# Another list of how many positions of each step are summed by twos, in a graph layer on one core

## The chip, the core and the metric

The kernel runs on one core of a Trainium2 chip. The metric is the device time of one execution in microseconds (us), as the median of several runs. The profile is of one further execution.

## What is computed

The reference normalizes the node features, sums the attributes of the edges that arrive at each node, and puts both through two dense layers:

```
h = maximum(layernorm(x), 0)                       # x: 12500 x 128
agg = segment_sum(edge_attr, dst)                  # 412500 x 48 -> 12500 x 48, dst sorted
z = relu(concat([h, agg, globals_of_graph_0]) @ W1 + b1)      # 256 hidden
out = x + z @ W2 + b2                              # 12500 x 128
```

All is in float32. The edges are 79 MB and make up most of what is read.

## The kernel before

**Steps.** The sorted edges are cut into chunks of CE = 896 (128 partitions x T = 7 positions). CS = 8 chunks make a step; there are NS = 58 steps, 57 full ones and a last short one. A step has two halves of CH = 4 chunks. For each chunk and position a one-hot matrix says which of W = 32 nodes near the chunk's start each edge belongs to. VectorE makes these matrices (`onehot`, line 312), two steps ahead (EARLY = 2).

**Sums.** `aggregate(s, h, twos)` multiplies, on TensorE, one-hot matrix by edge attributes, and adds the results up in PSUM (`ps`). A position of a half can be taken in two ways. One by one: four products, each with a 32-column stationary operand and 48 moving columns, each into its own 32 partitions. By twos: two products, each with the one-hot matrices of two neighbouring chunks as a 64-column stationary operand and the attributes of both as 96 moving columns; two of the four blocks that come out are wanted, the others are not read. The program issues 56 products for a step with no position by twos and 28 for one with all 14 by twos; the trace records two matmuls and two weight loads for a product, so 112 and 56.

**Levels.** `LEVELS[s]`, line 608, says how many of the step's 14 positions (7 in each half) are taken by twos:

```
twos = [max(0, LEVELS[s] - T), min(T, LEVELS[s])]     # first half, second half
```

So up to 7 the second half alone is concerned, and within a half the last positions are. Where a half has any, `keep_sums` (line 360) makes two further small copies on ScalarE besides the usual one, since the second chunk of a pair has its sums in the other 48 columns.

**What follows a step's sums.** ScalarE copies them to SBUF (`sums`). `place_columns` makes on VectorE a matrix that says where each of the 128 rows belongs among the nodes, `place` multiplies on TensorE (`pp`), and `add` adds on VectorE into the node sums `aggT` (line 391). Blocks of up to 512 nodes whose sums are complete go through the two layers in pieces (`turn`, `first_h`, `first_a`, `relu`, `second`, `result`, `store`), which a planner with costs spreads over half-steps (`piece`, `at`). The planner does not look at LEVELS: the order of all engines is written out under a manual schedule and is the same for any list.

**Loads.** Each step has four loads of edges of 336 KB (`load(s, i)`, line 144 issues them on SyncE's queue). `few` makes each of them wait until the load FLIGHT = 5 places before it has landed, and until the product that TensorE was given last at that point of the program is done. They are issued three steps ahead (AHEAD = 4). Loads of node rows (`xt`) and of indices (`di`) go through the same rule.

Of the kernel before, what the change touches and what calls it, by code (L numbers as in the profile page):

```python
# [22 lines left out]
def kernel(  # L23
# [134 lines left out]
    with fast:  # L158
# [175 lines left out]
        def aggregate(s, h, twos):  # L334
            left = s == NSF and h
            if h == 0:
                banks_s[s] = ps_agg.tile([P, 512], F32, name="ps")[:, :4 * DE].rearrange("p (h f) -> p h f", h=2)
            ps, es, oh = banks_s[s], edges[s], onehots[s]
            n = TT if left else T
            for t in range(n):  # L340
                first, end = t == 0 and h == 0, t == n - 1
                if t >= n - twos:
                    for q in range(0, CH, 2):
                        c = CH * h + q
                        product(ps[W * q:W * (q + 2), h], oh[:, c // 2, t], both[s][c // 2][:, :, t * DE:(t + 1) * DE],
                                start=first, stop=end, skip_group_check=True)
                    continue
                for q in range(1 if left else CH):
                    c = CH * h + q
                    o = DE * (q % 2) if twos else 0  # L350
                    product(
                        ps[W * q:W * (q + 1), h, o:o + DE], oh[:, c // 2, t, c % 2], es[c][:, t * DE:(t + 1) * DE],
                        start=first, stop=end, skip_group_check=True)
# [32 lines left out]
        def add(s):  # L386
            _, v = nc.values_load_multi_w_load_instructions(  # L387
                at_i[0:1, s:s + 1], engines=[DVE], min_val=low(s), max_val=high(s),
                skip_runtime_bounds_check_because="clamped to these on the chip")
            to = aggT[:HI + DE, ds(v[0], WG)]  # L390
            nc.vector.tensor_tensor(to, to, banks_p.pop(s)[:HI + DE, :WG], OP.add)  # L391
# [213 lines left out]
        FLIGHT = 5  # L605


        LEVELS = (0, 0, 0, 0, 7, 0, 0, 9, 14, 3, 14, 14, 0, 14, 3, 3, 2, 0, 5, 14, 0, 14, 2, 3, 0, 4, 14, 0, 14, 2, 4, 0, 3, 0, 5, 14, 0, 14, 0, 4, 0, 2, 0, 3, 14, 0, 14, 4, 2, 2, 0, 2, 2, 4, 0, 0, 0, 0)
        LATE = NS - 7
        NEAR = len(FIRST) + 1  # L610
        with tc.manual_schedule():
# [242 lines left out]
            for s in range(NS):  # L854
# [27 lines left out]
                if s >= LATE:  # L882
                    for p in now:
                        place(p)
                        add(p)
                twos = [max(0, LEVELS[s] - T), min(T, LEVELS[s])]
                aggregate(s, 0, twos[0])
# [175 lines left out]
```

## Time and profile before

| | |
|---|---|
| median of 3 runs | 300.12 us |
| the runs | 300.12, 307.49, 296.84 us |
| the profiled execution | 298.43 us |
| its span, first to last instruction | 296.6 us |
| mean granted TensorE clock | 0.991 |
| moved by DMA | 95.19 MB, 321 GB/s mean |

How to read it: PE is TensorE's products, PEld its weight loads, DVE VectorE, ACT ScalarE, POOL GpSimd, SP SyncE. A row names line, engine, operation, output and inputs. Every product of the kernel is issued through one helper, so its line is L195, and the tile name tells them apart: `ps` are the sums by one-hot matrices, `pp` the placement, `ph` the first layer, `po` the second, `pt` transposes. "issue" as the end of a wait means that the profile shows nothing that the engine waited for. The clock is the share of TensorE's full clock that was granted.

### The profile page before, as it was taken

To read this page: it belongs to the slowest core of one execution; us is meant where nothing else is said; L and a number is where in the kernel's file an instruction comes from. 1 tells how busy PE (TensorE), PEld (TensorE's weight loads), DVE (VectorE), ACT (ScalarE), POOL (GpSimd) and SP (SyncE) were. 2 spreads that over 40 slices of the span, in tenths; PEclk is the share of its full clock that TensorE was granted. 3 is DMA by queue.
4 is the path that set the end of the run, shared out by engine and by line. 5 is a ranking of instruction groups with operands and counts; after the bars stand their busy time and mean duration, and the time that the engine had idled before them with its cause. 6 is when DMAs were issued, how large, how long until landed. Compare 5 with 4: busy or idle time off the path is not lost.

```text
span 296.6 us, 15062 instructions
## 1 busy us (share of the span) xinstructions
PE 283.1 (95%) x6553; PEld 223.5 (75%) x6554; DVE 237.0 (80%) x537; ACT 161.0 (54%) x399; POOL 73.7 (25%) x88
## 2 busy tenths in 40 slices
PE   6799897999999999999999999999999999999992
PEld 2657666898878778878878788867877977787781
DVE  6838969699998997887978699698986799986222
ACT  3477557323756664743666458644651985664420
POOL 3032381130212563021022212021111022103720
PEclk9999998999999999999999999999999999999998
DMA  6999999999999999999999999999999999999962
GB/s 162 372 314 345 272 358 313 370 370 370 356 357 356 326 367 285 298 348 290 332 312 339 346 345 317 336 321 322 310 347 337 353 298 323 337 352 317 363 222 81
DMA packets 69815, 95.19 MB, mean 321 GB/s; under 512 B 5018, under 2 KB 64739, under 8 KB 69743
## 3 DMA queue, kind: packets, MB, share of 16 engines
q1 hardware_dynamic: 67583, 87.66, 89.1%
q0 software_dynamic: 2160, 6.50, 6.1%
q8 instruction: 53, 0.87, 1.2%
q14 instruction: 19, 0.16, 0.1%
HBM read 87.74 MB, written 6.40 MB: 317 GB/s over the span
## 4 chain that ended last, share of the span: by engine, by line
PE 81%; DVE 8%; ACT 3%; DMA 2%; issue 2%; SPq 1%; DVEq 1%
PE ps L195 30%; PE ph L195 21%; PE po L195 14%; PE pp L195 10%; PE pt L199 5%; DVE oh L312 3%; DMA e<-in_edge_attr_dram 2%; DVE place L374 2%; ACT xn L438 1%; ACT hT L452 1%; PE pt L195 1%; DVE st L408 1%; DVE aggT L391 1%; DVE ph L489 1%; DVEq L387 1%
## 5 line engine op out<-in xcount | busy, mean ns | idle before, releaser
L312 DVE TENSOR_TENSOR oh<-iota,rel 128x1792 f32<-128x1792 f32 (+1 forms) x60 | 120.5, 2009 | 0.4 <-ACT rel L270 0.4
L195 PEld LDWEIGHTS ps<-e,oh 128*32 128x32 f32 (+1 forms) x5448 | 94.7, 116 | 21.7 <-issue 5.8
L195 PE MATMUL ps<-e,oh 128*32 128x48 f32 (+1 forms) x5448 | 106.5, 217 | 3.1 <-issue 1.2
L360 ACT COPY sums<-ps 128x192 f32<-128x192 f32 (+2 forms) x129 | 36.7, 285 | 78.7 <-PE ps L195 76.8
L431 POOL TENSOR_TENSOR xb<-xt,b_sb 128x512 f32<-128x512 f32 (+1 forms) x21 | 34.2, 1630 | 131.7 <-DVE aggT L533 79.4
L195 PE MATMUL ph<-hT,w1h 128*128 128x512 f32 (+2 forms) x100 | 49.6, 602 | 0.1
L195 PE MATMUL po<-w,hid 128*128 128x128 f32 (+1 forms) x376 | 48.0, 281 | 0.9 <-ACT hid L516 0.9
L516 ACT ACTIVATE hid<-ph,bias 128x512 f32<-128x512 f32 (+2 forms) x49 | 30.4, 670 | 30.4 <-PE ph L195 22.9
L195 PEld LDWEIGHTS po<-w,hid 128*128 128x128 f32 (+1 forms) x376 | 45.1, 196 | 2.0 <-ACT hid L516 1.3
L391 DVE TENSOR_TENSOR aggT<-aggT,pp 112x246 f32 x58 | 23.6, 406 | 24.5 <-PE pp L195 18.2
L195 PE MATMUL pp<-place,sums 128*112 128x128 f32 x232 | 39.0, 291 | 0.2 <-DVE place L374 0.2
L195 PEld LDWEIGHTS pp<-place,sums 128*112 128x112 f32 x232 | 28.9, 176 | 7.1 <-issue 1.7
L438 ACT ACTIVATE xn<-xt,sh,sc 128x128 f32<-128x128 f32 x80 | 33.1, 483 | 0.3
L374 DVE TENSOR_TENSOR place<-iota,pos 128x256 f32<-128x256 f32 x58 | 32.9, 569 | 0.0
L195 PE MATMUL ph<-aggT,w1a 48*128 48x256 f32 (+1 forms) x192 | 28.6, 402 | 0.2 <-DVE aggT L391 0.2
L195 PEld LDWEIGHTS ph<-aggT,w1a 48*128 48x128 f32 x192 | 17.2, 186 | 10.1 <-issue 6.8
L452 ACT COPY hT<-pt 128x512 f32<-128x512 f32 (+1 forms) x22 | 23.0, 1044 | 3.2 <-PE pt L199 3.1
L195 PEld LDWEIGHTS ph<-hT,w1h 128*128 128x128 f32 x100 | 16.7, 196 | 7.1 <-issue 4.6
L533 DVE TENSOR_TENSOR aggT<-po,xb 128x512 f32<-128x512 f32 x16 | 11.0, 685 | 9.2 <-PE po L195 9.2
L541 POOL DMA_DIRECT2D out_dram<-ot x9 | 5.0, 553 | 51.6 <-DVE ot L533 43.7
L408 DVE BATCH_NORM_STATS2 st<-xt 128x6 f32<-128x128 f32 x80 | 17.3, 277 | 0.0
L199 PE MATMUL pt<-ident,xn 128*128 128x128 f32 x84 | 14.1, 289 | 0.0
(137 smaller groups left out, 188.1 us busy)
## 6 DMA issues: line engine op xcount, KB each, us to landing
e<-in_edge_attr_dram SPq DMA_DIRECT2D x230, 336.0 KB, 5.2
xt<-in_x_dram SPq DMA_DIRECT2D x19, 256.0 KB, 4.9
out_dram<-aggT POOLq DMA_DIRECT2D x16, 256.0 KB, 4.5
out_dram<-ot POOLq DMA_DIRECT2D x7, 256.0 KB, 4.8
di<-in_dst_dram SPq DMA_DIRECT2D x3, 448.0 KB, 5.3
aggT<-in_x_dram SPq DMA_DIRECT2D x4, 256.0 KB, 4.2
xt<-in_x_dram SPq DMA_DIRECT2D x2, 128.0 KB, 4.6
out_dram<-ot SPq DMA_DIRECT2D x2, 128.0 KB, 3.3
```

Source lines behind the costliest of these rows:

```text
L195: last[:] = [nc.tensor.matmul(*a, **k).ins.name]
L199: last[:] = [nc.tensor.transpose(*a, **k).ins.name]
L312: nc.vector.tensor_tensor(to, iota[:, None, :W].to_broadcast([P, n, W]), r[:, :, None].to_broadcast([P, n, W]), OP.is_equal)
L360: nc.scalar.copy(to[k, h], ps[k, h, None, o:o + DE].to_broadcast([k.stop - k.start, h.stop - h.start, 2, DE]))
L374: nc.vector.tensor_tensor(po, iota[:, None, :WP].to_broadcast([P, 2, WP]), pos[:, s, :, None].to_broadcast([P, 2, WP]), OP.is_equal)
L391: nc.vector.tensor_tensor(to, to, banks_p.pop(s)[:HI + DE, :WG], OP.add)
L408: nc.vector.bn_stats(st[:m, q, :], xs[j][:m, q, :])
L431: nc.gpsimd.tensor_tensor(xb[:m, :r], xs[j][:m, :r], b2_sb[:m, None, :].to_broadcast([m, r, D]), OP.add)
L438: nc.scalar.activation(xn[:m, q], xs[j][:m, q], AF.Relu, bias=shift[j][:m, q:q + 1], scale=scale[j][:m, q:q + 1])
L452: nc.scalar.copy(hT[:, :m * r].rearrange("d (p r) -> d r p", r=r), ht[j][:, :m * r].rearrange("d (r p) -> d r p", r=r))
L516: nc.scalar.activation(to, ph, AF.Relu, bias=bias[:, h:h + 1])
L533: nc.vector.tensor_tensor(ot[:m, :r], pos_o[j][:m, :r], xbs[j][:m, :r], OP.add)
```

## The change

One tuple is replaced. Nothing else is touched.

```diff
-        LEVELS = (0, 0, 0, 0, 7, 0, 0, 9, 14, 3, 14, 14, 0, 14, 3, 3, 2, 0, 5, 14, 0, 14, 2, 3, 0, 4, 14, 0, 14, 2, 4, 0, 3, 0, 5, 14, 0, 14, 0, 4, 0, 2, 0, 3, 14, 0, 14, 4, 2, 2, 0, 2, 2, 4, 0, 0, 0, 0)
+        LEVELS = (0, 0, 0, 0, 11, 4, 14, 3, 14, 14, 0, 14, 3, 2, 0, 2, 0, 0, 3, 0, 2, 0, 2, 0, 1, 3, 0, 0, 0, 3, 0, 0, 1, 0, 3, 0, 4, 0, 14, 0, 14, 4, 2, 3, 0, 0, 2, 0, 14, 0, 14, 5, 2, 4, 1, 2, 1, 0)
```

The sum of the list goes from 248 to 185. Steps with any position by twos go from 35 to 33, steps with all 14 from 12 to 8, and mixed steps (1 to 13) from 23 to 25. By stretches of steps:

| steps | positions by twos before | after |
|---|---|---|
| 4 to 9 | 33 | 60 |
| 10 to 36 | 148 | 43 |
| 37 to 57 | 67 | 82 |

## The prediction

> **What bounds the kernel now.** I read the page first (busy shares, the 40 slices, the chain that ended last), then stretches of time with the granted clock, then what SyncE's queue waited for, and last the chain of waits in a few windows, to price one step's sums.
>
> ```profile
> PE 283.1 (95%) x6553; PEld 223.5 (75%) x6554; DVE 237.0 (80%) x537; ACT 161.0 (54%) x399; POOL 73.7 (25%) x88
> DMA  6999999999999999999999999999999999999962
> q8 instruction: 53, 0.87, 1.2%
> PE 81%; DVE 8%; ACT 3%; DMA 2%; issue 2%; SPq 1%; DVEq 1%
> e<-in_edge_attr_dram SPq DMA_DIRECT2D x230, 336.0 KB, 5.2
> ```
>
> Two resources are full at once: TensorE is busy for 95% of the span, and the DMA engines show 9 in 37 of 40 slices. The chain follows TensorE, so TensorE looks like the bound. Stretches of time (length; busy time of PE, PEld, DVE, ACT and POOL; clock; DMA share; GB/s) say the same of the middle:
>
> ```profile
> 45.70:49.10 3.40, 1.81 (x52) 1.44 (x40) 3.40 (x7) 1.83 (x4) 0.33 (x1) 1.00 0.96 314
> 49.10:52.60 3.50, 3.50 (x54) 3.27 (x53) 3.50 (x4) 2.47 (x8) 0.74 (x2) 0.51 0.93 291
> 140.00:185.00 45.00, 45.00 (x1067) 35.88 (x1071) 38.13 (x84) 28.65 (x71) 8.66 (x7) 1.00 1.01 333
> 185.00:230.00 45.00, 45.00 (x1132) 35.54 (x1120) 37.15 (x76) 20.99 (x50) 6.64 (x6) 1.00 0.99 329
> ```
>
> From 140 to 230 us TensorE has no idle time. But the loads are no freer. A load of edges waits until the fifth load before it has landed, and until TensorE has reached a named product. The queue's waits show which of the two binds:
>
> ```profile
> SPq L144 <- DMA e<-in_edge_attr_dram: 108.2, 176, 2.4
> SPq L144 <- PE pp L195: 6.5, 15, 1.1
> ```
>
> 176 of the 230 loads were let go by the landing of an edge load; the largest group let go by a product is 15. So the loads run as one closed stream that TensorE hardly paces, and sums by twos fill TensorE's time beside it. The question is how far TensorE runs behind its data, since only that much can be won by lightening TensorE.
>
> **The price of a position.** Steps around 110 to 120 us in the chain (start, length, matmul records):
>
> ```profile
> 110.06 1.33 PE ps L195 x112
> 114.23 2.46 PE ps L195 x56
> 119.03 1.64 PE ps L195 x104
> ```
>
> Level 0 takes 1.33 us with 112 records, level 14 takes 2.46 us with 56. So a position by twos costs (2.46 - 1.33) / 14 = 0.081 us more, although it saves 4 matmul records and as many weight loads. Level 2 (x104) took 0.31 us more, not 0.16: a mixed step pays 0.15 us once. The new list has 63 positions fewer (5.1 us less) and 25 mixed steps for 23 (0.3 us more): 4.8 us less work on TensorE. The order of all else stays.
>
> ScalarE copies twice more in each step that has any twos, 33 steps for 35, four copies fewer; at 54% busy it hides them. VectorE, GpSimd and SyncE issue the same instructions in the same order. VectorE (45-us stretches with 37 to 38 us busy) has room for the few microseconds by which TensorE may come earlier.
>
> **Steps 4 to 9.** Levels 11, 4, 14, 3, 14, 14 replace 7, 0, 0, 9, 14, 3: 27 positions more, 27 x 0.081 = 2.2 us. They land where TensorE stood idle:
>
> ```profile
> 41.46 0.29 PE L195 MATMUL ps<-e,oh 128*32 128x48 f32 x8 [0.35 <-issue]
> 46.86 0.37 PE L195 MATMUL ps<-e,oh 128*32 128x48 f32 x13 [0.81 <-issue]
> 48.62 3.28 PE L195 MATMUL po<-w,hid 128*128 128x128 f32 x16 [0.77 <-ACT hid L516]
> 59.02 1.95 PE L195 MATMUL po<-w,hid 128*128 128x128 f32 x16
> ```
>
> That is 1.93 us idle. Right behind it the clock was 0.51 for 3.5 us (second stretch above), and 16 products that take 1.95 us at 59.02 took 3.28. With steps 5 and 6 fuller the idle time closes and the clock should hold: 3.5 x 0.49 = 1.7 us come back. TensorE would gain 1.93 + 1.7 - 2.2 = 1.4 us here. I carry none of it, because the next part caps what TensorE gains before step 37.
>
> The Trainium skill's page "TensorE: Matmul & The Clock Gate" (HAM oscillation) asks for no idle gap over about 3.4 us; by it no gap here would lower the clock. The trace decides otherwise: the longest gap above is 0.81 us, and the clock fell after a stretch with 1.81 of 3.40 us busy. By the page the new waits below cost only themselves; by the row, a stretch half idle can cost 1.7 us more, which the range takes in.
>
> **Up to step 37: the data bind.** Steps 4 to 36 hold 78 positions fewer: 78 x 0.081 = 6.3 us. How much can TensorE use? Step 37's sums, and the last of its four loads (the 152nd of 230):
>
> ```profile
> 188.12 2.53 PE L195 MATMUL ps<-e,oh 128*64 128x96 f32 x56
> L144 SPq DMA_DIRECT2D e<-in_edge_attr_dram x1: 502/502/502, 182.3 to 182.3; - x1
> DMA to landing us min/median/max: 4.8/4.8/4.8
> ```
>
> It landed at 182.3 + 4.8 = 187.1. Step 37 now has level 0, and its second half, which needs this load, comes 1.33 / 2 = 0.7 us after its start: it can start at 186.4, 1.7 us sooner than 188.1. The other 4.6 of the 6.3 us become waits for edges in steps 10 to 36, in the place of the work. What queues behind such a wait on TensorE is the same step's placement and the layer's products; VectorE's additions then come as late as those.
>
> **The stream itself.** Fewer twos mean more instructions, and TensorE's instructions come over the same DMA engines: 53 packets of 0.87 MB in all (16 KB each) for 6553 + 6554 records, one for about 250. Their time is 1.2% x 16 x 296.6 / 53 = 1.07 us each on one engine. One began at 113.4, and the load issued just before it:
>
> ```profile
> L144 SPq DMA_DIRECT2D e<-in_edge_attr_dram x1: 367/367/367, 113.3 to 113.3; - x1
> DMA to landing us min/median/max: 6.4/6.4/6.4
> q8 instruction: 1, 0.02, 2.3%
> ```
>
> It took 6.4 us against a median of 5.2: the packet held up the stream by about its own length. Each position not taken by twos adds 8 records. Up to step 37 that is 78 x 8 / 250 = 2.5 packets, 2.5 x 1.0 = 2.5 us of stream; for the whole list 63 x 8 / 250 = 2.0. The bounds of one packet are 0 (wholly beside the loads) and 1.2 us (6.4 - 5.2); I take 1.0, nearest to its own 1.07. So step 37 starts -1.7 + 2.5 = +0.8 us against before.
>
> The Trainium skill's page "Runtime: NRT & Kernel Launch" (Instruction fetch mechanics) calls crossing a 16 KB block of instructions mostly hidden; then step 37 starts 1.7 us early. The load at 113.3 speaks against it; it is the first rival below.
>
> **From step 37 to the end.** The list has 15 positions more here (-63 against -78) and one mixed step more: 15 x 0.081 + 0.15 = 1.4 us. The tightest place is step 51:
>
> ```profile
> 253.73 1.71 PE L195 MATMUL ps<-e,oh 128*32 128x48 f32 x104
> L144 SPq DMA_DIRECT2D e<-in_edge_attr_dram x1: 368/368/368, 247.8 to 247.8; - x1
> DMA to landing us min/median/max: 5.2/5.2/5.2
> ```
>
> Its last load (the 208th) landed at 253.0 and binds 0.7 us into the step: 252.3, 1.4 us of room. Later by 70 x 8 / 250 = 2.2 packets it would start at +0.8; TensorE's own way from step 37 gives +0.8 + 8 x 0.081 = +1.4 there. TensorE binds. Sum: 0.8 + 1.4 = +2.2 us.
>
> The profiled execution took 298.4 us (span 296.6 and 1.8 around it): 300.6. The median of the runs shown is 300.1, 1.7 us above; on it the forecast is 302.3 us.
>
> **The rivals.**
>
> First, the instruction packets cost the loads nothing. Then -1.7 + 1.4 = -0.3 us: 298.1 on the profile, 299.8 on the median. For it: one engine in sixteen is held. Against: the load at 113.3. Chance 0.2.
>
> Second, TensorE is the bound after all and takes all the relief: 4.8 us of work less, 1.93 us of idle time filled and 1.7 us of clock regained, -8.4 us: 290.0 on the profile, 291.7 on the median, faster by 2.8%. For it: 45.00 of 45.00 us busy. Against: the landings of step 37 and step 51, 1.0 and 0.7 us ahead of the sums. It decides only if the stream too comes over 6 us sooner, and nothing in the change hastens it. Chance 0.06.
>
> Third, slower: TensorE runs out of instructions. At 41.46 and 46.86, in steps 5 and 6, both at level 0, it stopped for 0.35 and 0.81 us within its sums, with "issue" as what ended it and not a landing, and the clock drop followed: 1.2 + 1.7 = 2.9 us for the group. The new list puts low steps in rows at 15 to 17, 20 to 24, 26 to 28 and 30 to 33. The waits for edges up to step 37 (4.6 us, and 2.5 more with the later stream) would swallow 7.1 us of such stops. Four groups are 11.6 us: 2.2 + 11.6 - 7.1 = 6.7 us, 306.8 on the median. Three give 303.9, so it decides from the fourth group on, or sooner where one falls behind step 37 (44 and 45 are both at 0) and nothing swallows it. Against: from 140 to 230 us TensorE stood still nowhere (45.00 of 45.00), with a dozen steps at level 0 or 2 among them. Chance 0.16.
>
> **How the numbers follow.** Within 2% (294.1 to 306.1; about what a measurement of this kernel can tell, its three runs lying between 296.8 and 307.5) lie my forecast, 0.58, and the first rival, 0.2: 0.78. Faster 0.06, slower 0.16. The likeliest time is 302.3. The range reaches down to 296.5 (the first rival, less the 3.3 us by which the fastest run shown lies below the median) and up to 307.0 (the forecast, two clock drops of 1.7 us that nothing absorbs and 2.5 x 0.2 us for packets at their upper bound make 306.2; the third rival's 306.8 is taken in, its worse ends are not).
>
> **What would show it.** Right: a shorter busy time of TensorE by some 5 us, idle stretches that end with a landing of edges between 100 and 150 us, 55 instruction packets, a clock near 1.00 at 49 to 53 us, and sums of step 37 starting within 1 us of the landing of its last load. Wrong: TensorE still without idle time and the span shorter by over 3 us (second rival); gaps inside the sums of steps at level 0 to 3 that no landing ends, with a clock of 0.5 behind them (third); an end before 299 us with 55 packets (first).

## The result, and the profile after

| | before | after |
|---|---|---|
| median of 6 runs each | 299.38 us (296.84 to 307.49) | 307.78 us (305.36 to 308.90) |
| ratio, with 95% interval | | 1.031 (1.024 to 1.038) |
| profiled execution, its span | 298.43 us, 296.6 us | 307.25 us, 305.4 us |

The changed kernel is slower by 3.1%, 5.5 us above the forecast and 0.8 us above the range. Ratios here leave out disturbed runs, so they can differ a little from the quotient of two medians.

From the page of the changed kernel: busy times, instruction packets, the chain that ended last, and the groups of TensorE's sums and of the second layer.

```profile
PE 281.6 (92%) x6805; PEld 218.7 (72%) x6806; DVE 236.4 (77%) x537; ACT 158.5 (52%) x395; POOL 74.6 (24%) x88
q8 instruction: 55, 0.90, 1.2%
PE 81%; issue 6%; DVE 4%; ACT 3%; DMA 2%; SPq 1%; DVEq 1%
L195 PE MATMUL ps<-e,oh 128*32 128x48 f32 (+1 forms) x5700 | 103.0, 214 | 6.4 <-issue 4.9
L195 PE MATMUL po<-w,hid 128*128 128x128 f32 (+1 forms) x376 | 48.7, 279 | 5.9 <-issue 4.6
```

The same two groups in the kernel before:

```profile
L195 PE MATMUL ps<-e,oh 128*32 128x48 f32 (+1 forms) x5448 | 106.5, 217 | 3.1 <-issue 1.2
L195 PE MATMUL po<-w,hid 128*128 128x128 f32 (+1 forms) x376 | 48.0, 281 | 0.9 <-ACT hid L516 0.9
```

TensorE is busy for 1.5 us less than before (283.1), and the span is 8.8 us longer, so its idle time grew by 10.3 us, from 13.5 to 23.8. The chain shows where to look: "issue", time in which the engine waited for nothing that the profile shows, rose from 2% to 6%. What TensorE waited for, in the changed kernel (total, times, longest; rows that differ little between the kernels are left out):

```profile
PE ps L195 <- issue: 4.9, 8, 1.3
PE po L195 <- issue: 4.6, 6, 1.3
PE ps L195 <- DMA e<-in_edge_attr_dram: 1.4, 3, 0.5
PE pt L195 <- issue: 1.2, 1, 1.2
PE ph L195 <- DVE ot L533: 0.6, 1, 0.6
PE ph L195 <- issue: 0.2, 1, 0.2
```

and in the kernel before:

```profile
PE ps L195 <- issue: 1.2, 2, 0.8
PE ps L195 <- DMA e<-in_edge_attr_dram: 0.9, 2, 0.5
```

Stops by "issue" went from 2 (1.2 us) to 16 (4.9 + 4.6 + 1.2 + 0.2 = 10.9 us), that is +9.7. With the 0.6 us put down to VectorE, which falls in the same pattern, as shown next, that is the 10.3 us; all other waits together changed by less than 1 us. Waits for edges, which the forecast expected to grow by 4.6 us, grew by 0.5.

**What the stops have in common.** I numbered all records of TensorE in order of start: matmuls, weight loads, and the 133 of its sequencer, semaphores for the most part, which the busy counts leave out. All 16 stops, and the one put down to VectorE (at 99.43), stand at a count that leaves 192 when divided by 256, to within three records. So do the two of before, at 41.46 and 46.86. (Why 192, the traces don't show.) Three in a row in the changed kernel (start, length, operation, idle time before):

```profile
140.22 1.35 PE L195 MATMUL ps<-e,oh 128*32 128x48 f32 x106 [0.38 <-issue]
...
145.00 1.32 PE L195 MATMUL ps<-e,oh 128*32 128x48 f32 x105 [0.67 <-issue]
...
149.69 0.38 PE L195 MATMUL po<-w,hid 128*128 128x128 f32 x1 [0.64 <-issue]
```

The first two stand inside the sums of a step each, the third inside a second layer. What they share is the distance (length; busy time and records of PE and PEld, the other engines; clock; DMA):

```profile
140.22:145.00 4.78, 4.11 (x127) 2.78 (x127) 4.75 (x12) 2.71 (x7) 0.68 (x1) 1.00 1.01 338
145.00:149.69 4.69, 4.05 (x129) 3.79 (x128) 4.17 (x16) 2.01 (x4) 0.00 (x0) 1.00 1.02 339
```

With two semaphore instructions more in the first stretch, and one record less at an edge of the second, 127 + 127 and 129 + 128 are 256 instructions each, one 16 KB packet. The packets of the instruction queue that belong to them are found by narrow windows, here 137.7 to 137.8, 142.5 to 142.6 and 147.3 to 147.4 us; each row is the packet that began there, and its time as a share of 16 engines for 0.1 us:

```profile
q8 instruction: 1, 0.02, 62.8%
...
q8 instruction: 1, 0.02, 59.5%
...
q8 instruction: 1, 0.02, 58.2%
```

They took 0.628 x 16 x 0.1 = 1.00, 0.95 and 0.93 us, so they ended at 138.8, 143.5 and 148.3, and TensorE went on 1.4 to 1.5 us later each time. The next packet began 2.3 us after TensorE had gone on (140.22 to 142.55, 145.00 to 147.35). 2.3 + 0.95 + 1.45 = 4.7 us is the whole period here. A block that TensorE can do in 4.1 us takes 4.7, and TensorE stops at its end. Over all 17 stops the time from packet's end to going on is 1.25 to 1.6 us. The period is less fixed: the packet begins 1.9 to 3.6 us after TensorE passed the block end before (median 2.7), and the block before a stop takes 4.6 to 6.0 us (median 5.2).

The strongest sign takes in all block ends, with or without a stop. I paired packets and block ends one by one, in order. No block end is passed sooner than 1.25 us after its packet ended, in either kernel. In the kernel before 4 of 50 are passed within 1.65 us of it, the median being 2.9; in the changed kernel 26 of 52. So the packet is not merely a load on the DMA engines, as the prediction's sum had it: TensorE waits for it. And packets do not run ahead: in the changed kernel each begins from 1.3 us ahead of the passing of the block end before to 3.6 us behind it.

How near the limit each kernel is can be read from one window, 140 to 190 us, first before, then after:

```profile
140.00:190.00 50.00, 50.00 (x1197) 40.13 (x1199) 42.57 (x92) 31.39 (x75) 8.66 (x7) 1.00 1.01 333
```

```profile
140.00:190.00 50.00, 45.93 (x1365) 36.10 (x1364) 41.12 (x91) 26.30 (x63) 9.22 (x7) 1.00 0.96 312
```

Before, 1197 + 1199 records pass in 50 us, 5.3 us for 256. After, 1365 + 1364 pass, 4.7 us for 256, which is the period above, and 4.07 us are idle. It is no sharp limit: eleven single blocks of the kernel before went by in 3.3 to 4.7 us without a stop.

**Where it is lost.** The sums of step 9 start 2.1 us earlier than before (58.83 for 60.90), those of step 16 1.8 us earlier (88.27 for 90.09), those of step 37 4.3 us later and those of step 57 8.7 us later (290.34 for 281.66). The early steps gained, steps 16 to 37 lost 6.1 us and the rest 4.4 us. The data were there. Step 37's last load and its sums, in the changed kernel:

```profile
L144 SPq DMA_DIRECT2D e<-in_edge_attr_dram x1: 367/367/367, 182.0 to 182.0; - x1
...
DMA to landing us min/median/max: 5.3/5.3/5.3
```

```profile
192.43 0.38 PE L195 MATMUL ps<-e,oh 128*32 128x48 f32 x16
194.06 0.63 PE L195 MATMUL ps<-e,oh 128*32 128x48 f32 x41 [1.26 <-issue]
```

It landed at 187.3, 0.2 us later than before, and was first needed over 5 us after that.

### The profile page after: what moved, and what is told of

Read it like the earlier page. It is cut to its first block, busy times and chain, and to the rows that moved or that the text cites. A ratio compares the mean times of both kernels' runs of the same rounds, so it can differ in the third digit from the quotient of the medians.

```text
span 305.4 us, 15564 instructions
## 1 busy us (share of the span) xinstructions
PE 281.6 (92%) x6805; PEld 218.7 (72%) x6806; DVE 236.4 (77%) x537; ACT 158.5 (52%) x395; POOL 74.6 (24%) x88
## 4 chain that ended last, share of the span: by engine, by line
PE 81%; issue 6%; DVE 4%; ACT 3%; DMA 2%; SPq 1%; DVEq 1%
PE ps L195 30%; PE ph L195 21%; PE po L195 15%; PE pp L195 10%; PE pt L199 4%; DMA e<-in_edge_attr_dram 2%; DVE place L374 1%; PE pt L195 1%; ACT xn L438 1%; ACT hT L452 1%; ACT hid L516 1%; DVE oh L312 1%; DVE ot L533 1%; SPq L144 0%; DVEq L387 0%
## 5 line engine op out<-in xcount | busy, mean ns | idle before, releaser
L195 PEld LDWEIGHTS ps<-e,oh 128*32 128x32 f32 (+1 forms) x5700 | 90.3, 114 | 26.0 <-issue 8.8
L195 PE MATMUL ps<-e,oh 128*32 128x48 f32 (+1 forms) x5700 | 103.0, 214 | 6.4 <-issue 4.9
L360 ACT COPY sums<-ps 128x192 f32<-128x192 f32 (+2 forms) x125 | 35.3, 284 | 91.3 <-PE ps L195 89.8
L431 POOL TENSOR_TENSOR xb<-xt,b_sb 128x512 f32<-128x512 f32 (+1 forms) x21 | 35.2, 1675 | 138.7 <-DVE aggT L533 99.3
L195 PE MATMUL po<-w,hid 128*128 128x128 f32 (+1 forms) x376 | 48.7, 279 | 5.9 <-issue 4.6
L374 DVE TENSOR_TENSOR place<-iota,pos 128x256 f32<-128x256 f32 x58 | 31.1, 538 | 0.0
L195 PE MATMUL ph<-aggT,w1a 48*128 48x256 f32 (+1 forms) x192 | 29.3, 404 | 0.8 <-DVE ot L533 0.6
L195 PEld LDWEIGHTS ph<-aggT,w1a 48*128 48x128 f32 x192 | 17.2, 186 | 11.5 <-issue 8.4
L533 DVE TENSOR_TENSOR aggT<-po,xb 128x512 f32<-128x512 f32 x16 | 11.0, 687 | 11.5 <-PE po L195 11.5
```

Source lines behind the costliest of these rows:

```text
L195: last[:] = [nc.tensor.matmul(*a, **k).ins.name]
L360: nc.scalar.copy(to[k, h], ps[k, h, None, o:o + DE].to_broadcast([k.stop - k.start, h.stop - h.start, 2, DE]))
L374: nc.vector.tensor_tensor(po, iota[:, None, :WP].to_broadcast([P, 2, WP]), pos[:, s, :, None].to_broadcast([P, 2, WP]), OP.is_equal)
L431: nc.gpsimd.tensor_tensor(xb[:m, :r], xs[j][:m, :r], b2_sb[:m, None, :].to_broadcast([m, r, D]), OP.add)
L533: nc.vector.tensor_tensor(ot[:m, :r], pos_o[j][:m, :r], xbs[j][:m, :r], OP.add)
```

## The experiments

Theory S (supply): TensorE's instructions come in blocks of 256, at most about one ahead; where TensorE uses a block up in less than about 4.7 us it stops at the block's end, so the time depends on how many records there are and on which of them share a block. Theory D (data and array): the edge stream and the array's own work bind, as in the sum on record, and the stops are a by-product. A third possibility, that the old list is simply better in itself wherever the block ends fall, came up on the way.

| run | list and change | median, us | ratio (95%) | stops by "issue", us |
|---|---|---|---|---|
| early | new list in steps 0 to 15, old after | 301.75 | 1.007 (1.000 to 1.014) | 5, 3.4 |
| late | old list in steps 0 to 15, new after | 307.66 | 1.016 (1.005 to 1.027) | 17, 13.3 |
| zero | no position by twos | 322.60 | 1.074 (1.065 to 1.083) | 34, 33.8 |
| apart | old list, 116 of its pairs as two half-wide products each | 315.95 | 1.051 (1.040 to 1.061) | 9, 9.1 |
| spread | 185 positions, otherwise placed | 304.04 | 1.007 (0.999 to 1.015) | 13, 11.6 |
| paced | 251 positions, placed by block | 302.29 | 0.996 (0.990 to 1.001) | 3, 2.8 |
| flight4 | new list, 4 loads in flight | 331.68 | 1.088 (1.073 to 1.102) | none |
| flight8 | old list, 8 loads in flight | 305.51 | 1.016 (1.009 to 1.023) | 9, 8.0 |
| grid | new list, 64 records put ahead | 321.99 (one run) | - | 22, 21.3 |
| gridold | old list, 64 records put ahead | 312.70 | 1.038 (1.022 to 1.054) | 15, 11.8 |
| grid256 | new list, 256 records put ahead | 311.41 | 1.027 (1.010 to 1.044) | 19, 15.3 |

Stops (number, total) are those of the profiled execution of each, which can lie some microseconds off its median.

**Which part of the list.** The two halves of the change, alone:

```diff
 late:  LEVELS = old[0:16] + new[16:58]
 early: LEVELS = new[0:16] + old[16:58]
```

> The old list up to step 15, the new one from step 16 on. Theory (instruction supply): a block of 256 of TensorE's instructions comes no sooner than some 4.8 us after the block before it was entered, so low levels in a row make TensorE stop at block ends; the stops of the new list lie at steps 16 to 37, so this kernel keeps them: 306 to 311 us, with ten or more stops ended by issue. Rival (later stream of edges, as forecast): 300 to 303, waits ended by landings. Rival (the longer sums in steps 4 to 9 are the loss): 298 to 300.

> The new list up to step 15, the old one from step 16 on. Instruction supply: stops only up to step 16 or so (two or three, 1 to 2 us), and the idle time and the low clock near 46 to 52 us are gone: 296 to 300 us, no different from before or up to 1% faster. Rival (steps 4 to 9 are the loss): 306 to 309. Rival (later stream of edges): 299 to 301.

Late loses about half of the 3.1% by its ratio (1.005 to 1.027). Early, expected between no change and 1% faster, is at 1.000 to 1.014. The intervals overlap, so the times alone do not split the loss. The stops do: 16 of late's 17 lie from step 16 on. Both lists have 81 positions in steps 0 to 15, so late has the changed kernel's records and block ends from step 16 on, and ten of its stops stand at the very block ends where the changed kernel stops. So most stops come from steps 16 on, where positions were taken away, and not from the 27 added in steps 4 to 9. For the same reason early has the instructions and block ends of before from step 16 on; yet it has 5 stops there (3.4 us), where before has none. So the place of the block ends is not all: it also matters when TensorE reaches an end and when its packet comes. Which of the two made these five is not shown, nor how much the number of stops varies between executions of one kernel.

**More supply needed, less array work.** All levels at zero:

```diff
-        LEVELS = (0, 0, 0, 0, 7, 0, 0, 9, 14, 3, ...)
+        LEVELS = (0,) * 58
```

> No position by twos anywhere: TensorE has 248 x 0.08 = 20 us less to do than before and some 2000 instructions more, 59 blocks for 51. Instruction supply: 53 blocks at 4.8 us from 41 us on end at 295, and the ends of steps need 10 us more: 305 at the least, 310 to 318 with blocks that no stop makes up for. Rival (TensorE's time decides): under 295. Rival (later stream of edges): 8 packets of 1 us less 2 us of room, 304 to 306, with waits ended by landings.

```profile
PE 272.4 (85%) x7545; PEld 212.6 (66%) x7546; DVE 236.9 (74%) x537; ACT 140.6 (44%) x329; POOL 72.7 (23%) x88
PE 77%; issue 12%; ACT 5%; DMA 2%; DVE 1%; SPq 1%; DVEq 0%; ACTq 0%
```

```profile
PE ps L195 <- issue: 32.4, 33, 3.3
PE ps L195 <- DMA e<-in_edge_attr_dram: 1.9, 3, 1.1
```

TensorE is busy for 10.7 us less (20 were expected; for 20 us in four stretches its clock is at half, which lengthens the work), the waits for edges are 1.9 us, and the kernel is 7.4% slower, with 33.8 us of stops. At 322.6 us it is above the 310 to 318 expected. Theory D has nothing to put this down to. A window far from the start shows the limit again: 1315 + 1313 records in 50 us, 4.9 us for 256.

```profile
100.00:150.00 50.00, 45.76 (x1315) 34.95 (x1313) 39.35 (x83) 22.49 (x53) 17.79 (x13) 1.00 0.98 323
```

The attempt at the converse, more records at the same array work, failed:

```diff
+    for v in (0, 1) if apart_ else (None,):   # one half of the 96 columns each
-        product(ps[W * q:W * (q + 2), h], oh[:, c // 2, t], both[...][:, :, ...], ...)
+        product(ps[W * q:W * (q + 2), h, cols], oh[:, c // 2, t], both[...][:, two, ...], ...)
```

> The old list, and TensorE's array time with it, but in steps 10 to 36 the 116 positions by which the old list exceeds the new one are issued as twice as many products of half as many moving columns: as many instructions as one by one, 928 records more. Instruction supply: stops at every second or third end of a block of 256 in steps 10 to 36, 8 or more, step 37 starts near 192 us as in the new list: 303 to 309 us. Rival (TensorE's array time decides): 298 to 301, no change. Rival (instruction packets hold up the edges): 3.7 packets, 301 to 303, waits ended by landings.

```profile
PE 296.2 (93%) x7017; PEld 234.8 (74%) x7018; DVE 236.2 (74%) x537; ACT 161.5 (51%) x399; POOL 70.0 (22%) x88
```

The two halves cost the array more than the whole: a step with all 14 positions in halves took 3.51 us (118.34 and 143.45) for 2.53, that is 0.98 / 14 = 0.07 us a position. (The 13.1 us by which TensorE is busier than before hold 6.8 us at half clock near the end as well.) So the premise of equal array time was wrong, and the 5% says nothing of the supply. Only 2 of the 9 stops by "issue" fell in steps 10 to 36, where 8 or more were expected. The run tells the two theories apart no better than before it.

**Same number, other places.** If only the number of records counts, 185 positions give the same time wherever they are:

```diff
-        LEVELS = new                                 # 185, in the change's places
+        LEVELS = (0, 0, 0, 0, 0, 5, 0, 13, 2, 3, 6, 3, 3, 0, 12, 2, 2, 1, 0, 3, 3, 4, 12, 0, 0, 14, 0, 6, 1, 3, 2, 0, 0, 8, 5, 7, 0, 14, 0, 4, 0, 0, 5, 1, 0, 13, 5, 0, 11, 0, 5, 0, 5, 0, 0, 0, 2, 0)
```

> Again 185 positions by twos, as many products and instructions as the new list, but placed so that, with a block of 256 instructions every 5 us at best, hardly a block is used up sooner than that. Instruction supply: few stops ended by issue (under 4 us in all against 11.5), 299 to 303 us. Rival (the number of instructions or of packets counts, wherever they stand): 306 to 309 us as the new list.

It took 1.007 (0.999 to 1.015) of before, the change 1.031 (1.024 to 1.038), and the intervals don't meet. So most of the 3.1% hangs on where the positions are, and little on 63 fewer. The stops do not bear this out as expected: under 4 us were forecast, and the profiled execution, at 309.79 us the longest of its ten, has 13 (11.6 us) and 10 us at half clock. The reading rests on the times alone. The same bookkeeping, with a block at best every 5 us, then gave a list of its own:

> A list of 251 positions found with the same bookkeeping, as the best by it: TensorE's work, a block of 256 instructions at best every 5 us, and the edges' landings. Instruction supply: no stops, 296 to 300 us, up to 1% below before. Rival (before is at its floor for another reason, or the bookkeeping does not carry over): 300 to 304.

With 251 positions it is 0.996 (0.990 to 1.001): at 3 stops, where none was expected, as good as before, and not measurably better. It is the best list that these runs found, and no version beats the kernel before by more than its uncertainty.

**Loads in flight.** The packets share DMA engines with the loads, so fewer loads in flight might bring them sooner:

```diff
-        FLIGHT = 5
+        FLIGHT = 4      # flight4, with the new list;  8 in flight8, with the old list
```

> The new list with four loads in flight in place of five. If an instruction packet waits behind the loads' packets in the DMA queues, the time from the entry into a block to the next block shortens by up to the 0.9 us of one load, the stops shrink from 11.5 to some 3 us: 299 to 302 us. If the wait is fixed: 306 to 309, stops as before. If four loads are too few to keep the stream going: slower than 309, with waits ended by landings.

> The old list with eight loads in flight in place of five. If an instruction packet waits behind the loads' packets, the next block comes up to 2.7 us later, and most blocks stop TensorE: over 320 us. If the wait is fixed: 298 to 301 us, no stops.

Of the waits of TensorE with four in flight, and with eight:

```profile
PE ps L195 <- DMA e<-in_edge_attr_dram: 26.3, 35, 2.7
```

```profile
PE ps L195 <- issue: 5.2, 5, 2.3
```

With four, the stream starves TensorE (26.3 us) and no wait is left that ends by "issue": here the data do bind, and a kernel bound by its data looks quite different from the changed one. With eight, the old list has 9 stops in place of 2, and at them the packet begins 3.7 us (median) after TensorE passed the block end before, against 2.7 at the 17 stops of the changed kernel. That would fit packets held up by loads in flight. But gridold, below, has 3.1 with five loads in flight, so it is not shown; and the loss is some 5 us (1.6%) and not the over 20 that I expected. A repeat of this kernel gave 305.81 us, 1.012 (1.003 to 1.022), with 9 stops again.

**The decisive runs: move the grid.** Products whose result nothing uses, ahead of step 0, move every later product against the block ends. Beside the added products, only one more use of the buffers `ph` is new:

```diff
+            ph = ps_h.tile([P, 512], F32, name="ph")
+            for _ in range(16):          # 64 records; 64 times in grid256, 256 records
+                product(ph[:W, :1], ones[:, :W], iota[:, :1], start=True, stop=True)
```

> The new list, with 16 tiny products (64 matmul and weight-load records, 32 x 1 results that nobody reads) put in at the start, where TensorE waits for the first loads. Every later instruction stands 64 places further on in the blocks of 256. Instruction supply: the stops ended by issue lie again at one and the same place in the count of records modulo 256 (192), so elsewhere in the program than in the new list's run; 304 to 309 us. Rival (something in those steps makes TensorE wait): the stops keep their products, and their place modulo 256 moves on by 64, to 0.

> The kernel before with its own list of 248 positions, and 16 tiny products of the selector ahead of step 0, whose result nothing uses. They put 64 records (a quarter of a block of 256) ahead of every later product and change nothing else that TensorE does. If supply of TensorE's instructions sets the time and the list of before was merely well placed against the block ends, it loses its fit: more than the 2 stops of before, at record counts of 192 modulo 256, 8 or more of them, and about 305 to 315 us. If the list of before is better in itself, wherever the block ends fall, 299 to 302 us with 2 to 4 stops.

> The changed kernel with its own list of 185 positions, and 64 tiny products ahead of step 0, which are one whole block of 256 records. The block ends then fall between the same products of the same steps as in the changed kernel. If the place of the block ends against the list sets the time, this run shows the changed kernel's time again, 305 to 312 us with 14 to 20 stops, although four times as many products were added as in the shifted run of 322 us. If the added products themselves cost (a late start, a used accumulator), it is at or above those 322 us.

The shifted new list (grid):

```profile
PE ps L195 <- issue: 21.3, 22, 2.2
```

The shifted old list (gridold):

```profile
PE ps L195 <- issue: 11.8, 15, 1.4
```

The new list shifted by a whole block (grid256):

```profile
PE ps L195 <- issue: 8.7, 12, 1.5
PE po L195 <- issue: 3.2, 4, 1.6
```

In all three, the stops stand at counts of 192 modulo 256 again, although in the first two every product of the kernel has moved by 64. The old list, untouched, loses 3.8% by a quarter of a block; so it isn't better wherever the block ends fall, but fits them. 27 of its 51 block ends are now passed within 1.65 us of their packet, for 4 of 50 unshifted. The new list loses still more by the quarter block (322 us, in the one run there is, where 304 to 309 was expected: I had the place right and not the size; the clock was at half in three stretches of 3.4 us too). By a whole block, with four times as many added products, it is back at 1.027, against 1.031 unshifted, and 11 of its 19 stops stand at block ends of the changed kernel's stops. A late start is not the cause either: step 4 begins 1.7 us sooner in grid than unshifted, 0.5 us later in gridold and 3.4 us later in grid256. So it is not the added products that cost. No run shifted the old list by a whole block.

Early in the shifted old list the clock fell as well, from 35.8 to 42.6 us. A stop of 0.86 us, up to 36.53, stands at the start of that stretch, and a wait of 0.9 us for a load ahead of it:

```profile
34.00:38.00 4.00, 2.63 (x72) 2.43 (x74) 2.92 (x5) 0.31 (x1) 0.00 (x0) 0.73 1.01 310
38.00:42.00 4.00, 4.00 (x23) 2.39 (x20) 0.67 (x1) 1.22 (x4) 2.91 (x3) 0.50 1.04 362
```

## Why the prediction failed

- **"Up to step 37: the data bind"** is the step that failed. It read a load that landed 1.0 us ahead of step 37 as the limit and capped TensorE's gain at 1.7 us, the rest to "become waits for edges". No such waits came (+0.5 us in all). The load landed at 187.3, so the sums could have started at 186.6 and started at 192.43. TensorE was late, and not for want of data: what bound it was the supply of its own instructions, in the whole kernel 16 stops of 10.9 us and one of 0.6 us put down to VectorE.
- **The stream, +2.5 us.** 55 packets came, as forecast. But with two packets more by then (33 for 31), step 37's last load landed 0.2 us later, not 2.5. As far as this load shows, the packets cost the loads next to nothing, as the first rival had it; what they cost is at TensorE, in stops. The load at 113.3 that took 1.2 us more was no general price.
- **The third rival had the right mechanism, and the wrong cover and price.** It gave 306.8 us; the median is 307.8, and that the two are so near is luck. It counted 2.9 us for a group of two stops with a clock drop, and let waits for edges swallow 7.1 us. The runs show no swallowing, no clock drop in the changed kernel, and 17 stops of 0.7 us each on average (11.5 / 17). That it "stood still nowhere" from 140 to 230 was taken as evidence against. But the same rows had 5.4 and 5.1 us for each 256 records, only 0.7 and 0.4 above 4.7, where there is no margin; and the dozen low steps that it named are ten. Supply can't be saved up over several steps, since no packet of the changed kernel began more than 1.3 us ahead of the passing of the block end before; so rows of level 0 matter even where the mean over 50 us is enough.
- **From step 37 to the end, +1.4 us:** it is +4.4 (from 4.3 late to 8.7 late). Two stops fall here, 1.26 us at 194.06 and 1.21 at 241.70; with the 1.4 of work they make 3.9 of the 4.4.
- **TensorE's work, -4.8 us.** The group of sums fell by 3.5 us (106.5 to 103.0), TensorE as a whole by 1.5, although the clock drop of 1.7 us was gone. The size was right all the same. Step by step, level 0 takes 1.40 us, level 2 1.71 and level 14 2.53 in both kernels, and by such steps the new list is 4.8 us shorter. But a step with a stop inside counts 0.2 us more as busy (six steps at level 0: 1.60 to 1.66), and ten steps of the changed kernel are longer by 2.1 us in this way or beside a block end; those of before by 0.9, its clock drop included. That leaves 3.5. In the second layer, where six stops fall, the group rose by 0.7 us (48.0 to 48.7), although its own loss to the clock drop was gone; there the reason is not taken apart.
- **Right:** the idle time of the early steps and the clock drop close. In the changed kernel:

```profile
45.70:49.10 3.40, 3.10 (x57) 2.81 (x53) 3.40 (x7) 2.14 (x7) 0.35 (x1) 1.00 1.04 359
49.10:52.60 3.50, 3.50 (x117) 3.20 (x116) 3.50 (x4) 3.36 (x10) 0.73 (x2) 1.00 1.03 374
```

The clock is 1.00 from 49 to 53 us, and step 9 starts 2.1 us earlier.

The Trainium skill's page "Runtime: NRT & Kernel Launch" (Instruction fetch mechanics) says that the next block of 256 instructions is fetched while the current one runs, and that crossing a block is mostly hidden. The first half agrees with these traces: one packet for 256 of TensorE's instructions. The second holds for the kernel before (1.2 us of stops), and neither for the changed one (10.9 us) nor for the one with no position by twos (33.8 us).

What stays open is what decides when the next packet begins. Taken from the passing of the block end before, over all blocks, the median is 1.3 us in the kernel before, 2.0 with eight loads in flight and the same list, 2.0 in the changed kernel, and 2.4 in the shifted old list. I have no run that separates the queue's order from the moment of its request.

## What to carry to other kernels

Count TensorE's records, weight loads too, per microsecond, stretch by stretch: 256 in less than about 5 us, several times in a row, is a warning even where the engine shows no idle time. A wide product that wastes array time can pay by saving instructions: here a position by twos costs 0.081 us of array and saves 8 records, by estimate 8 / 256 x 4.7 = 0.15 us of supply, where supply binds. And a list tuned by trial may be tuned to where the block ends fall, so that an edit far ahead of it, even 16 idle products, undoes it.

## What the runs showed of the hardware

- TensorE's instructions come in packets of 256. In both kernels no block end was passed sooner than 1.25 us after its packet ended, and at the 17 stops of the changed kernel TensorE went on 1.25 to 1.6 us after it. In a row of stops, beside five loads in flight, a block took 4.7 us: 2.3 to the packet's start, 0.95 for it, 1.45 to going on. It is no fixed period: 4.6 to 6.0 us over the 17 stops.
- The stops carry no name of their own: "issue" in the waits, and in one case a VectorE instruction that had ended at 99.27, 0.2 us before TensorE went on. The place (192 modulo 256, with TensorE's semaphore instructions counted) gives them away.
- The clock falls beside some stops and not beside others: to 0.50 from 35.8 to 42.6 us in the shifted old list, after 3.45 us with 2.38 busy. In the changed kernel it stays at 1.00 up to 304.8 us, with 17 stops, though from 170.55 to 173.95 only 2.10 of 3.40 us are busy. The runs don't show where the limit lies.
- Two products half as wide cost the array 0.07 us a position more than one whole: 3.51 us for 2.53 in a step with all 14 positions.
